# A difference of states moved from VectorE to GpSimd, and other starting constants for a planner, in a four-layer graph network

## The chip, the cores and the metric

The kernel runs on one core of one Trainium2 chip. A time is the device time of one execution in microseconds. The core has a matrix engine (TensorE, PE in the profile, with its weight loads as PEld), a vector engine (VectorE, DVE), a scalar engine (ScalarE, ACT), a programmable vector engine (GpSimd, POOL), and DMA queues that are issued here by SyncE (SP) and ScalarE.

## The reference

There are 64 graphs of 256 nodes with 256 features (`x`) and a 0/1 adjacency matrix (`adj`, about 1.6% ones). Four residual layers follow one another; each normalises the rows and takes `relu`:

```
h = max(layernorm(x), 0);  x = x + GAT0(h, adj)       # 4 heads, softmax over neighbours, elu
h = max(layernorm(x), 0);  x = x + GAT1(h, adj)       # 4 heads, relu, residual, layernorm by head
h = max(layernorm(x), 0);  x = x + GAT2(h, adj)       # one head
h = max(layernorm(x), 0);  x = x + GRU(h, adj)        # three rounds:
    m = h @ weight[i];  aggr = A^T m
    r = sigmoid(W_ir aggr + W_hr h + b)               # and z alike
    n = tanh(W_in aggr + b + r * (W_hn h + b))
    h = (1 - z) * n + z * h
```

All arithmetic is fp32.

## The kernel before

**Units.** The graphs are worked on in 33 units: one graph, then 31 units of two graphs, then one graph (`units`, L854). For each unit `graphs` (L1080) records every operation of the four layers. Nothing is issued at this point: an operation is an entry with an engine, a cost in ns, the buffers that it reads and writes, and a function that emits it.

**The planner.** `_Schedule` (L546) then orders all operations of all units. `paths` (L651) gives each operation a first due time, from the end that its unit should have (PACE per two graphs, L520 and L1666) backwards: the due time of a successor, less STRETCH times that successor's cost, less MARGIN. `play` (L712) runs a simple model of the engines forward. On each engine the operation with the earliest due time among those that are ready goes first; a result is visible on another engine OVERLAP and HOP ns after the producer is free again (L562, L563); an operation marked `port=True` starts only when no other such operation, of VectorE or GpSimd, is running in the model. `latest` (L664) plays the same backwards from the starts of the forward play, and its start times are the due times of the next forward play. After seven plays (ROUNDS) the best order by the model's own span is issued (`run`, L791), with the order on each engine fixed. So four of the five changed numbers (PACE, HOP, STRETCH, MARGIN) have no instruction of their own: they decide which order comes out.

**Pools.** Buffers come from pools of fixed size (L891 to L902): 13 of "g" (128x512 fp32), 8 PSUM banks, 3 of "sw" and so on. The model reserves them in its order.

**The GRU of a unit of two graphs.** In each of its three rounds, `products` (L1550) forms the sums for the gates r and z of both graphs from seven products of 128x512 in place of eight. It needs four differences, each 128x512 fp32 with both inputs in SBUF, made by `less_of` (L1566) on VectorE at a planned cost of 700 ns:

- t1 = state of graph 1 less state of graph 0 (L1593), from the state `ht` alone
- t3 = aggregate of graph 1 less state of graph 1
- t2 = aggregate of graph 1 less t1
- t4 = aggregate of graph 0 less t2

t1 goes into t2 and into the product with `s[0]`; t2 into t4 and the product with `s[1]`. All matmuls of `products` carry line 1575, all differences line 1567. The aggregate `ag` is made from the same state: transposes (`rows_of`, L1491), a split into high and low parts on ScalarE (L1450) and VectorE, 16 matmuls for each half (L1463), and a copy on ScalarE. Units of one graph use `plain` (L1515) and have no such differences.

**GpSimd before.** It computes the powers of the normalisations (L1110 and L1111 for the rows, L1400 and L1401 for layer 1's heads), the caps of the adjacency (L1334) and a memset (L1232). At the start it also forms some products for score columns (`score_column`, L971, recorded at L912 through the helper `vec`).

Of the kernel before, what the change touches and what calls it, by code (L numbers as in the profile page):

```python
# [516 lines left out]
SCORE_MAX = 40.0  # L517
SLOPES = (0.2, 0.01, 0.2)
SPREAD = 3
PACE = 93600  # L520


def _runs(numbers):
# [22 lines left out]
class _Schedule:  # L546
# [13 lines left out]

    ENGINES = ("pe", "act", "dve", "pool", "sp")
    OVERLAP = {"pe": 0, "act": 90, "dve": 80, "pool": 0, "sp": 0}  # L562
    HOP = {"pe": 370, "act": 240, "dve": 240, "pool": 270, "sp": 0}  # L563
    DMA_LATENCY = 2000
    DMA_RATE = 220.0
    DMA_AHEAD = 2000
    STRETCH = 3.79
    MARGIN = 500
    ROUNDS = 7

    def __init__(self, tc, pools):
# [8 lines left out]
    def buf(self, cls, shape, dtype=F32, tile=None):  # L580
        return _Buf(cls, shape, dtype, tile)

    def op(self, engine, cost, emit, reads=(), writes=(), takes=(), nbytes=0, port=False):
        o = _Op()
        o.engine, o.cost, o.port, o.emit, o.group, o.nbytes = engine, cost, port, emit, self.group, nbytes
        o.index, o.succs, o.preds, o.bufs, o.takes = len(self.ops), [], set(), [], []
        for written, items in ((False, reads), (True, writes)):
            for item in items:
                b, part = item if isinstance(item, tuple) else (item, None)
                if b not in o.bufs:  # L590
                    o.bufs.append(b)
                    b.users += 1
                if written and not b.const and b not in o.takes:
                    o.takes.append(b)
                keys = list(b.parts) if part is None else [k for k in (part, None) if k in b.parts]
                for k in keys:
                    writer, readers = b.parts[k]
                    if writer is not None:
                        o.preds.add(writer)
                    if written:  # L600
                        o.preds.update(readers)
                writer, readers = b.parts.get(part, (None, []))
                if written:
                    if part is None:
                        b.parts.clear()
                    b.parts[part] = (o.index, [])
                else:
                    b.parts[part] = (writer, readers + [o.index])
        for b in takes:
            if not b.const and b not in o.takes:  # L610
                o.takes.append(b)
        o.preds.discard(o.index)
        for p in o.preds:
            self.ops[p].succs.append(o)
        self.ops.append(o)
        return o
# [28 lines left out]
    def lag(self, o, s):  # L645

        if o.nbytes:
            return self.DMA_LATENCY + o.nbytes / self.DMA_RATE
        return 0 if o.engine == s.engine == "pe" else self.OVERLAP[o.engine] + self.HOP[o.engine]

    def paths(self):  # L651

        due = {}
        for o in reversed(self.ops):
            late = self.end[o.group]
            for s in o.succs:
                if s.group == o.group or o.group < 0:
                    late = min(late, due[s.index] - self.STRETCH * s.cost - self.MARGIN)
            if o.nbytes:
# [52 lines left out]
    def play(self, due):  # L712
# [10 lines left out]
        def post(t, kind, o):  # L723
            nonlocal count
            count += 1
            heapq.heappush(events, (t, count, kind, o))
# [17 lines left out]
        while True:  # L744
# [25 lines left out]
            while events and events[0][0] == clock:  # L770
                _, _, kind, o = heapq.heappop(events)
                if kind == "free":
# [5 lines left out]
                    else:  # L778
                        post(clock + self.OVERLAP[o.engine] + self.HOP[o.engine], "done", o)
                    if o.engine == "pe":  # L780
# [30 lines left out]
def _fast_path(  # L811
# [34 lines left out]
    nc = tc.nc  # L846
# [56 lines left out]
    buf, op = sched.buf, sched.op  # L903
# [4 lines left out]
    def bank(dtype=F32):  # L908
        return buf("bank", [P, S * 4 // mybir.dt.size(dtype)], dtype)

    def vec(fn, cost, *args, reads=(), writes=(), engine="dve", port=False, **kw):
        emit = lambda: fn(*[a() if callable(a) else a for a in args], **kw)  # L912
        op(engine, cost, emit, reads, writes, port=port)
# [7 lines left out]
    def dma(engine, nbytes, emit, reads=(), writes=(), takes=()):  # L921
        return op(engine, 450 if engine == "sp" else 320, emit, reads, writes, takes, nbytes)
# [157 lines left out]
    def graphs(u, first, nb):  # L1080
# [5 lines left out]
        def part_of(fixed):  # L1086
            return lambda cost: fixed + (cost - fixed) * nb / 2

        pe, act, dve, pool = part_of(0), part_of(200), part_of(130), part_of(130)
# [351 lines left out]
        def gru(pair):  # L1441
# [63 lines left out]
            ht = transposed(hn, "ht3_")  # L1505
# [3 lines left out]
            for i in range(L):  # L1509
# [40 lines left out]
                def products(i, ht, ag, wi):  # L1550

                    of = lambda b, g: b.tile[:, :, g * N : (g + 1) * N]
                    p1, t1, t2, t3, t4 = (buf("g", [P, DC, N]) for _ in range(5))
                    turn = buf("turn", [P, 1])
                    ps_s, ps_t, ps_w = (bank() for _ in range(3))
                    s = {}  # L1560
                    for k in (1, 0, 2):
                        s[k] = buf("sw", [P, DC, D])
                        o = dma("sp", 1 << 18, lambda k=k: nc.sync.dma_start(s[k].tile, sd[i][k]), [(B_sd, (i, k))], [s[k]])
                        sched.after(o, "sw")

                    def less_of(out, x_, y_, reads, takes=()):  # L1566
                        return op("dve", 700, lambda: nc.vector.tensor_tensor(  # L1567
                            out.tile, x_(), y_(), op=OP.subtract), reads, [out], takes, port=True)

                    def product(ps, w, B_w, view, reads, first=False, last=False):  # L1570

                        def emit():
                            for j in range(DC):
                                for dc in range(DC):
                                    nc.tensor.matmul(  # L1575
                                        ps.tile[:, j * N : (j + 1) * N],
                                        lhsT=w()[:, dc, j * P : (j + 1) * P], rhs=view()[:, dc],
                                        start=(first and j == 0 and dc == 0), stop=(last and dc == DC - 1),
                                        skip_group_check=True,
                                    )  # L1580

                        op("pe", 1725, emit, [reads, B_w], [ps])

                    def kept(out, ps):
                        vec(nc.scalar.copy, 600, lambda: out.tile.rearrange("p j n -> p (j n)"), lambda: ps.tile,
                            reads=[ps], writes=[out], engine="act")

                    def added(out, ps, also=()):
                        vec(nc.vector.tensor_tensor, 700, lambda: out.tile,
                            lambda: ps.tile.rearrange("p (j n) -> p j n", j=DC), lambda: out.tile,  # L1590
                            op=OP.add, reads=[ps, *also], writes=[out])

                    less_of(t1, lambda: of(ht, 1), lambda: of(ht, 0), [ht])  # L1593
                    product(ps_s, lambda: whh[:, :, Z_], B_whh, lambda: of(ht, 0), ht, first=True)
                    kept(p1, ps_s)
                    sched.after(less_of(t3, lambda: of(ag, 1), lambda: of(ht, 1), [ht, ag], [turn]), "turn")
                    less_of(t2, lambda: of(ag, 1), lambda: t1.tile, [t1, ag])
                    less_of(t4, lambda: of(ag, 0), lambda: t2.tile, [t2, ag])
                    product(ps_w, lambda: s3, B_s3, lambda: t3.tile, t3, first=True)
                    kept(t3, ps_w)  # L1600
                    product(ps_s, lambda: s[1].tile, s[1], lambda: t2.tile, t2)
                    kept(t2, ps_s)
                    product(ps_s, lambda: s[0].tile, s[0], lambda: t1.tile, t1)
                    added(t3, ps_s)
                    product(ps_w, lambda: wi[:, :, R_], B_wc, lambda: t4.tile, t4, last=True)
                    added(t2, ps_w, [turn])
                    product(ps_t, lambda: wi[:, :, Z_], B_wc, lambda: of(ag, 0), ag, first=True, last=True)
                    added(p1, ps_t)
                    product(ps_s, lambda: s[2].tile, s[2], lambda: of(ag, 1), ag, last=True)
                    return (t2, t3), p1, ps_s  # L1610
# [43 lines left out]
                ht = h_new  # L1654
# [9 lines left out]
    for u, (first, nb) in enumerate(units):  # L1664
        sched.group = u
        sched.end[u] = (first + nb) * PACE / 2  # L1666
        graphs(u, first, nb)
# [3 lines left out]
    sched.group = U  # L1671
    sched.end[U] = sched.end[-1] = (B / 2 + 1) * PACE
    good, bad = buf("rs", [P, 64]), buf("rs", [P, 1])
# [66 lines left out]
```

## Time and profile before

| | |
|---|---|
| median of three runs | 3055.6 us (3054.23 to 3055.82) |
| the profiled execution, its own time | 3056.75 us |
| its span, first to last instruction | 3054.7 us |
| mean granted TensorE clock | 0.993 |
| L1567 VectorE g<-ht (t1) | 93 operations, mean 681 ns, 63.3 us in all |
| L1567 VectorE, the other differences | 93 of g<-ag,ht and 186 of g<-ag,g, mean 680 ns |
| GpSimd, two-input operation 128x256 fp32 at the start | 684 to 728 ns |
| GpSimd, power operation 128x4 and 128x8 | mean 1130 and 1757 ns |

The times of rows come from one profiled execution. The mean of a row is the length of one instruction; neighbouring instructions on an engine overlap somewhat, so that VectorE's operations of 680 ns follow each other every 600 ns. "Idle before" in a row is time in which that engine had nothing running just before instructions of the row, and the arrow names what ended it. The helper `vec` records many operations under line 912, so they are told apart by the names of their buffers.

### The profile page before, as it was taken

What the parts mean: (1) busy time and instruction counts of PE and PEld (TensorE: products, weight loads), DVE (VectorE), ACT (ScalarE), POOL (GpSimd) and SP (SyncE); (2) the same over time, 40 slices, a digit from 0 to 9 for tenths busy, and PEclk for the clock granted to TensorE, in tenths of its full rate; (3) what the DMA queues carried; (4) which work ended last, traced back from release to release, by engine and by line L of the source; (5) the groups of instructions that cost most, each with busy time, mean ns of one, the idle gap of its engine ahead of it and who ended that gap; (6) DMA issues with size and microseconds to landing.
All of it is one profiled execution on the core that took longest, in us unless ns stands there. A gap on an engine that the chain in (4) does not pass through costs nothing.

```text
span 3054.7 us, 56348 instructions
## 1 busy us (share of the span) xinstructions
PE 3000.5 (98%) x20900; PEld 2370.9 (78%) x20900; DVE 2533.0 (83%) x5933; ACT 2109.2 (69%) x4811; POOL 430.3 (14%) x643
## 2 busy tenths in 40 slices
PE   8799999999999999999999999999999999999998
PEld 7677787777787777787777787777777777787777
DVE  7876878888988888988888988888988888988764
ACT  7676667767776767766767766767776766766554
POOL 3311101111111111111111111111111111101100
PEclk9899999999999999999999999999999999999999
DMA  4111222221222122222121222221222221121110
GB/s 139 59 50 47 69 67 90 61 81 59 81 81 77 60 80 60 80 81 76 61 80 58 82 81 73 63 81 56 84 80 70 66 81 57 60 79 56 45 49 24
DMA packets 150936, 212.43 MB, mean 70 GB/s; under 512 B 49239, under 2 KB 102013, under 8 KB 143229
## 3 DMA queue, kind: packets, MB, share of 16 engines
q1 hardware_dynamic: 146752, 207.40, 21.7%
q8 instruction: 167, 2.74, 0.4%
q10 hardware_dynamic: 3900, 1.34, 0.2%
q14 instruction: 117, 0.95, 0.1%
HBM read 180.62 MB, written 19.68 MB: 66 GB/s over the span
## 4 chain that ended last, share of the span: by engine, by line
PE 95%; DVE 2%; ACT 1%; DMA 1%; issue 0%; POOL 0%; SPq 0%; ACTq 0%; DVEq 0%
PE bank L1575 37%; PE bank L1477 23%; PE bank L1267 12%; PE bank L1158 11%; PE bank L1463 6%; PE bank L1136 4%; PE bank L1491 3%; PE bank L1195 1%; DVE pt L912 1%; DVE g L912 0%; DVE o L912 0%; PE bank L1211 0%; PE bank L1032 0%; ACT g L912 0%; DMA xt<-in_x_dram 0%
## 5 line engine op out<-in xcount | busy, mean ns | idle before, releaser
L912 ACT ACTIVATE g<-g,bg 128x256 f32<-128x256 f32 (+1 forms) x756 | 393.9, 555 | 164.4 <-DVE g L912 96.6
L912 DVE SCALAR_TENSOR_TENSOR pt<-pt,f,cap 128x256 f32<-128x256 f32 x1152 | 476.2, 479 | 11.9 <-ACT pt L1248 10.1
L1248 ACT ACTIVATE pt<-cb,f 128x256 f32<-128x256 f32 x1062 | 441.3, 504 | 4.2 <-PE bank L1267 3.7
L1267 PEld LDWEIGHTS bank<-wh,pt 128*64 128x64 f32 (+1 forms) x8704 | 345.5, 141 | 85.5 <-issue 62.3
L1267 PE MATMUL bank<-wh,pt 128*64 128x65 f32 (+1 forms) x8704 | 391.3, 233 | 6.5 <-DVE pt L912 2.7
L912 DVE TENSOR_TENSOR g<-bank,g 128x512 f32<-128x512 f32 x279 | 191.4, 686 | 241.6 <-PE bank L1575 234.3
L1477 PE MATMUL bank<-ht,whh 128*128 128x512 f32 (+1 forms) x888 | 379.4, 561 | 0.0
L1477 PE MATMUL bank<-ag,wc 128*128 128x512 f32 (+1 forms) x888 | 377.9, 558 | 0.1
L1575 PE MATMUL bank<-g,sw 128*128 128x256 f32 x1488 | 349.8, 381 | 2.7 <-DVE g L1567 2.7
L912 DVE SCALAR_TENSOR_TENSOR g<-g,g 128x512 f32<-128x512 f32 (+1 forms) x396 | 257.2, 670 | 80.7 <-ACT g L912 80.5
L1575 PEld LDWEIGHTS bank<-g,sw 128*128 128x128 f32 x1488 | 278.7, 190 | 44.9 <-issue 4.5
L912 ACT ACTIVATE g<-bank,bg 128x256 f32<-128x256 f32 (+1 forms) x408 | 224.6, 568 | 108.3 <-PE bank L1477 97.6
L912 ACT COPY g<-bank 128x512 f32<-128x512 f32 x279 | 162.6, 583 | 187.8 <-PE bank L1575 181.9
L1477 PEld LDWEIGHTS bank<-ag,wc 128*128 128x128 f32 x888 | 164.4, 190 | 129.1 <-issue 120.1
L1477 PEld LDWEIGHTS bank<-ht,whh 128*128 128x128 f32 x888 | 161.1, 190 | 122.3 <-issue 103.6
L1463 PE MATMUL bank<-am_r,hl 128*128 128x256 f32 x1536 | 233.7, 301 | 0.0
L1119 ACT ACTIVATE xn<-xt,mv 128x256 f32<-128x256 f32 x384 | 210.5, 597 | 24.6 <-DVE mv L912 22.9
L1463 PEld LDWEIGHTS bank<-am_r,hl 128*128 128x128 f32 x1536 | 196.2, 189 | 31.8 <-issue 21.7
L1101 DVE BATCH_NORM_STATS2 st<-xt 128x6 f32<-128x256 f32 x512 | 207.9, 406 | 10.1 <-DMA xt<-in_x_dram 9.9
L912 ACT COPY ht<-bank 128x512 f32<-128x512 f32 (+1 forms) x264 | 143.4, 575 | 101.5 <-PE bank L1136 101.3
L1110 POOL TENSOR_SCALAR mv<-mv 128x4 f32<-128x4 f32 (+1 forms) x132 | 48.3, 366 | 1152.1 <-DVE mv L1102 1029.6
L1575 PE MATMUL bank<-ht,whh 128*128 128x256 f32 x744 | 180.2, 386 | 0.4 <-ACT ht L912 0.4
(113 smaller groups left out, 5389.9 us busy)
## 6 DMA issues: line engine op xcount, KB each, us to landing
sw<-sd SPq DMA_DIRECT2D x279, 256.0 KB, 2.7
cb<-rd SPq DMA_DIRECT2D x58, 1024.0 KB, 4.7
xt<-in_x_dram SPq DMA_DIRECT2D x31, 512.0 KB, 4.0
at<-in_adj_dram SPq DMA_DIRECT2D x31, 512.0 KB, 3.8
out_dram<-xt SPq DMA_DIRECT2D x31, 512.0 KB, 2.9
cb<-rd SPq DMA_DIRECT2D x29, 256.0 KB, 3.3
sd<-g SPq DMA_DIRECT2D x9, 256.0 KB, 2.3
cap<-cap_n SPq DMA_TRANSPOSE x128, 2.3
```

Source lines behind the costliest of these rows:

```text
L912: emit = lambda: fn(*[a() if callable(a) else a for a in args], **kw)
L1101: nc.vector.bn_stats(st.tile[:, c, :], xt.tile[:, c, :])
L1110: nc.gpsimd.tensor_scalar(mv.tile[:, 2, :], mv.tile[:, 1, :], 1e-5, None, op0=OP.add)
L1119: op("act", 610, lambda: nc.scalar.activation(xn.tile[:, c, :], xt.tile[:, c, :], AF.Relu, bias=mv.tile[:, 3, c : c + 1], scale=mv.tile[:, ...
L1136: nc.tensor.transpose(ps.tile[:, c * P : (c + 1) * P], xn.tile[:, c, dc * P : (dc + 1) * P], ident)
L1158: nc.tensor.matmul(ps.tile[:, : heads * W], lhsT=ht.tile[:, dc, c * P : (c + 1) * P], rhs=we[:, dc].rearrange("p h w -> p (h w)"), start=( ...
L1248: op("act", 500, lambda: nc.scalar.activation(pt.tile[:, b, jc, :], source(h, b), AF.Exp, scale=slope - 1.0, bias=f.tile[:, 1, h, c : c + ...
L1267: nc.tensor.matmul(ps[q * Q : (q + 1) * Q], lhsT=pt.tile[:, b, jc, i0 : i0 + Q], rhs=wh.tile[:, h, 2 * b + jc, :w], start=(jc == 0), stop= ...
L1463: nc.tensor.matmul(ps.tile[:, b * N : (b + 1) * N], lhsT=hl.tile[:, k, 2 * b + sc, :], rhs=am.tile[:, 2 * b + sc, :], start=(k == 0 and sc ...
L1477: nc.tensor.matmul(ps.tile[:, :S], lhsT=w[:, dc, g * P : (g + 1) * P], rhs=v.tile[:, dc, :], start=(first and dc == 0), stop=(last and dc ...
L1491: nc.tensor.transpose(ps.tile[:, c * P : (c + 1) * P], ht.tile[:, j, c * P : (c + 1) * P], ident)
L1575: nc.tensor.matmul(ps.tile[:, j * N : (j + 1) * N], lhsT=w()[:, dc, j * P : (j + 1) * P], rhs=view()[:, dc], start=(first and j == 0 and d ...
```

## The change

One of the four differences (t1) is computed by GpSimd with a planned cost of 1290 ns; the other three stay on VectorE. Four constants of the planner are different.

```diff
-PACE = 93600
+PACE = 94400
...
-    HOP = {"pe": 370, "act": 240, "dve": 240, "pool": 270, "sp": 0}
+    HOP = {"pe": 340, "act": 210, "dve": 210, "pool": 240, "sp": 0}
...
-    STRETCH = 3.79
-    MARGIN = 500
+    STRETCH = 3.33
+    MARGIN = 800
...
-                    def less_of(out, x_, y_, reads, takes=()):
-                        return op("dve", 700, lambda: nc.vector.tensor_tensor(
+                    def less_of(out, x_, y_, reads, takes=(), engine="dve"):
+                        eng = nc.vector if engine == "dve" else nc.gpsimd
+                        return op(engine, 700 if engine == "dve" else 1290, lambda: eng.tensor_tensor(
                             out.tile, x_(), y_(), op=OP.subtract), reads, [out], takes, port=True)
...
-                    less_of(t1, lambda: of(ht, 1), lambda: of(ht, 0), [ht])
+                    less_of(t1, lambda: of(ht, 1), lambda: of(ht, 0), [ht], engine="pool")
```

## The prediction

> **What bounds the kernel now.** I read the page's busy shares first, then the stages, then who waits for whom.
>
> ```profile
> span 3054.7 us, 56348 instructions
> PE 3000.5 (98%) x20900; PEld 2370.9 (78%) x20900; DVE 2533.0 (83%) x5933; ACT 2109.2 (69%) x4811; POOL 430.3 (14%) x643
> ...
> PE 95%; DVE 2%; ACT 1%; DMA 1%; issue 0%; POOL 0%; SPq 0%; ACTq 0%; DVEq 0%
> ```
>
> TensorE is idle for 3054.7 - 3000.5 = 54.2 us in the whole span, and the chain that ended last is 95% TensorE. A matmul's end is modelled, so "busy" alone would not prove that TensorE is the limit. The view of stages says where the 54 us are (columns: stage, its length, busy time and instructions of each engine, granted clock, DMA share, GB/s):
>
> ```profile
> 0.00:86.00 86.00, 69.71 (x784) 60.83 (x784) 63.13 (x192) 60.69 (x170) 23.37 (x49) 1.00 0.43 124
> 86.00:108.00 22.00, 5.15 (x38) 3.47 (x39) 19.91 (x57) 4.67 (x10) 10.96 (x10) 0.54 0.04 14
> 108.00:206.00 98.00, 98.00 (x701) 80.29 (x701) 77.91 (x210) 77.22 (x188) 19.02 (x31) 0.98 0.22 68
> 206.00:350.00 144.00, 133.93 (x937) 107.55 (x938) 113.51 (x278) 87.53 (x206) 21.07 (x31) 0.96 0.21 64
> 350.00:2800.00 2450.00, 2449.93 (x17113) 1928.41 (x17113) 2086.58 (x4827) 1746.54 (x3958) 339.29 (x498) 1.00 0.23 72
> 2800.00:3047.00 247.00, 243.03 (x1330) 189.96 (x1328) 169.82 (x369) 132.53 (x283) 16.63 (x24) 0.99 0.12 36
> 3047.00:3055.00 8.00, 0.75 (x4) 0.40 (x4) 2.15 (x7) 0.00 (x0) 0.00 (x0) 0.72 0.33 108
> ```
>
> Idle of TensorE: 16.3 us before 86 (nearly all of it the first loads), 16.9 in 86 to 108, 10.1 in 206 to 350, 4.0 and 7.0 at the end. Between 350 and 2800 it is 0.07 us in 2450. The list of waits, restricted to TensorE and to 500 to 2780, comes back empty. The same pattern of matmuls comes round every 91.8 us there (76 matmuls of L1267 start at 1061.95, 1153.74 and 1245.55 in the chain), and that is the matmul work of a unit of two graphs: nothing but fewer or faster matmuls would shorten this part, and the change touches no matmul. So only the filling and the draining can gain. The filling has one large hole (timeline, TensorE then GpSimd; the bracket is the idle time before the piece and its releaser):
>
> ```profile
> 88.10 1.22 PE L1267 MATMUL bank<-wh,pt 128*64 128x65 f32 x16 [0.52 <-DVE pt L912]
> 104.12 2.80 PE L1136 MATMUL bank<-ident,xn 128*128 128x128 f32 x8 [14.80 <-ACT xn L1119]
> ...
> 86.06 0.20 POOL L1400 TENSOR_SCALAR mean<-mean 128x8 f32<-128x8 f32 x1 [10.27 <-DVE mean L912]
> ...
> 89.64 2.98 POOL L1400 TENSOR_SCALAR mean<-mean 128x8 f32<-128x8 f32 x1 [1.64 <-DVE mean L912]
> ```
>
> In the hole VectorE is 91% busy (19.91 of 22.00) with the second layer's normalisation of the first units, and TensorE waits for what follows from it. The last two lines are one instruction, 0.20 us and then 2.98 us: in the second case VectorE issued five operations with two SBUF inputs back to back (89.47 to 92.55 in its timeline), and GpSimd ended 0.1 us after them.
>
> **What the Trainium skill says.** "SBUF — State Buffer", section "Who interferes with whom": VectorE's second SBUF read port is GpSimd's only one; an operation of VectorE with two SBUF inputs and a GpSimd operation that reads SBUF exclude each other for whole instructions, and whoever starts first holds it. The 2.98 us agree. "GPSIMD Engine Reference", section 3.1: a two-input elementwise operation takes 4497 ns at 2048 fp32 elements, 2.2 ns each, about twice VectorE's. The trace agrees: 684 ns on GpSimd at 256 elements. "TensorE: Matmul & The Clock Gate", Part 1: after an idle window of some 3.4 us the clock is halved until TensorE has been busy for as long. The granted clock of 0.54 in 86 to 108 agrees, and 16 matmuls of L1158 take 5.86 us at 107.39 where they take 3.56 at 115.02: the hole costs 2.3 us more than its idle time.
>
> **The change, part by part.**
>
> *t1 to GpSimd.* Of the row "L1567 DVE TENSOR_TENSOR g<-ht ... x93 | 63.3, 681" all 93 leave VectorE. They start 0.60 us apart from the next operation (1383.18 to 1383.78), so VectorE gets back 93 x 0.60 = 56 us, 1.8 us per unit of 91.8. GpSimd gets 93 operations of 128x512. No row shows one; from 684 ns plus 256 x 2.2 ns I estimate 1.25 us, and the planner's 1290 ns lie beside it. That is 116 us more on GpSimd, 430 to 546 us, 18% of the span. While it holds the port, VectorE's two-input operations wait: at worst 1.25 us each time, 3.75 us per unit. VectorE therefore changes by -1.8 to +1.95 us per unit; it is busy 78.8 us in 500 to 592, so it ends between 77 and 81 of 92. TensorE stays the limit by 11 us per unit. In latency, t1 is 0.6 us longer alone and up to 3 us when the port is taken (the 2.98 above). What waits for t1 is t2 and then two products; t2 also needs the aggregate of the new state, which takes transposes, a split and 16 matmuls after the same state. At 1419.16 a t1 is done and the next t2 comes at 1427.60. So I take 0 for 350 to 2800. Bounds: nothing below 0, as TensorE has nothing to gain there; above, see the rival D. Behind a t1 in GpSimd's queue stand the power operations of the normalisations; they wait up to 1.25 us more, and in the full part other matmuls cover that.
>
> In 206 to 350, where TensorE waited 2.7 us for an L1567 operation and 2.8 for hl, four t1 stand: 4 x 0.60 = 2.4 us of VectorE. A third to a half is on TensorE's path: -1 us. In 86 to 108 there is no t1 (the first starts at 144.3): nothing.
>
> *HOP 30 ns lower.* This alters no instruction, only the planner's idea of a latency. It is safe when the chip is faster than the plan: a copy on ScalarE starts 0.19 us after the matmul slots of its group are over (68.99 against 67.93 + 4 x 0.217), and the plan had 0.37 and gets 0.34. So no new waits from it: 0.
>
> *PACE, STRETCH, MARGIN.* They set only the due times of the first of seven plays; from then on due times come from the previous order. An operation of cost c moves its predecessors' due time by 3.79c + 500 before and 3.33c + 800 after. The two are equal at 300 / 0.46 = 652 ns, which is a usual cost on VectorE: a matmul group of 1725 ns pulls 0.49 us less, one of 160 ns 0.23 us more. PACE moves the units' ends 0.8 us further apart per unit. So it is a small push to a procedure that settles into a different order. Direct cost 0; what it does is redraw the filling and the draining. Here I can't work out the order by hand, only what is at stake. To be gained: the hole (16.9 idle + 2.3 of slow clock), 10.1 in 206 to 350, about 4 before the end, and 1.9 of the last 7.0 (one wait, the rest is the last rows and their DMA): 35 us at most. To be lost: any number, in steps such as the one in rival C. For the hole: VectorE had 4 us free in 50 to 62 (7.76 of 12.00) and then was full from 74 on, and two of GpSimd's operations stood in the chain for 4.6 us with the port taken. An order that takes the first, single graph ahead, or spreads that normalisation, halves it. I put -9 on this, half of 19.2 rounded down, and nothing on the end.
>
> *Sum.* 0 (full part) - 1 - 9 + 0 = -10. Span 3054.7 - 10 = 3044.7. The profiled run took 3056.75, 2.05 more than its span; the median of the runs is 1.15 less than that one. 3044.7 + 2.05 - 1.15 = 3045.6, so **3046 us** as a median.
>
> **Rivals.**
>
> A, the forecast, faster by over 0.2%: between the bound (3049.5) and nearly all of the 35 us, 3025 to 3049. For it: there are 31 us that depend on order alone, and VectorE, relieved, is what the hole waits for. Against: the relief itself starts after the hole.
>
> B, a redrawn order with the same holes: 3050 to 3061, middle 3055. For it: the units' needs at the start are the same, so VectorE must do the early layers before TensorE has a GRU to fill with. Against: 20 us of holes rarely come out the same within 6.
>
> C, slower, the filling: one more normalisation of layer 1 comes ahead of what TensorE waits for. One half is nine VectorE operations at 0.60 and two GpSimd ones (0.54 + 1.76): 7.7 us, two halves 15.4. All of it is TensorE's idle time, as in 89 to 104. That gives 3071, and it decides once TensorE's ready work at about 90 us is used up, which in the profile before it was at 89.3. Seen against it: the planner knows these costs; for it: it knows nothing of GpSimd locked out for 2.98 us.
>
> D, slower, in the full part: t1 starves behind VectorE's runs of two-input operations, or stops them, and a product waits in every layer. If 0.65 us each time (1.25 - 0.60) were uncovered, 93 x 0.65 = 60 us: 3116. It needs the cushion of several us to be gone; the empty list of waits speaks against it.
>
> **How the numbers follow.** A measurement of this kernel tells a change from none at about 0.2%, 6.1 us (3049.5 and 3061.7 are the bounds). Chances: A 0.45, B 0.20, C 0.29, D 0.06. Faster 0.45, same 0.20, slower 0.35. The likeliest one's own range is 3030 to 3049. Both signs hold most of the chance, so the range reaches from 3028, below which I leave A's best tenth or so, to 3078, above which are D and the cases of C with more than three such halves.
>
> **What would show it.** Right: TensorE idle of about 44 us, the stage up to 350 shorter, the spacing of the pattern still 91.8 us, L1567 with 93 operations on GpSimd of 1.2 to 1.4 us by median. Wrong in the part on t1: waits of TensorE for a GpSimd or L1567 release in the middle, or GpSimd operations of 3 us there. Wrong in the part on the order: the hole near 90 us longer than 15, or a new hole in the last 250 us.

## The result and the profile after

The changed kernel takes 3042.85 us (median of five, 3041.36 to 3043.07) against 3055.54 us for the kernel before in the same comparison: a ratio of 0.9958, 95% interval 0.9946 to 0.9969. That is 12.7 us less; 3046 had been forecast. The span went from 3054.7 to 3041.3 us, so 13.4 us are to be found in the profile.

The busy shares on the page of the kernel after:

```profile
span 3041.3 us, 56441 instructions
PE 2994.3 (98%) x20900; PEld 2369.7 (78%) x20900; DVE 2505.3 (82%) x5840; ACT 2111.0 (69%) x4811; POOL 541.3 (18%) x736
```

93 instructions went from VectorE to GpSimd. TensorE's idle time fell from 54.2 to 47.0 us (span less busy), that is by 7.2. Its busy time fell by 6.2 although its 20900 matmuls are the same. The stages (stage, its length, busy time and instructions of each engine, granted clock, DMA share, GB/s), kernel after:

```profile
0.00:86.00 86.00, 69.62 (x743) 59.98 (x744) 59.34 (x186) 58.87 (x167) 22.26 (x49) 1.00 0.42 124
86.00:108.00 22.00, 6.53 (x79) 4.64 (x78) 20.20 (x56) 5.63 (x12) 7.83 (x8) 0.67 0.00 0
108.00:206.00 98.00, 98.00 (x701) 80.37 (x702) 82.56 (x221) 80.08 (x194) 23.64 (x36) 0.99 0.24 75
206.00:350.00 144.00, 141.14 (x1080) 113.37 (x1081) 113.04 (x276) 95.67 (x223) 24.37 (x32) 1.00 0.21 63
350.00:2800.00 2450.00, 2449.52 (x17040) 1932.04 (x17037) 2073.55 (x4772) 1748.25 (x3960) 437.37 (x582) 1.00 0.22 72
```

Read against the same stages before, idle time is length less the first busy number. In 206 to 350 it is 2.9 us where it was 10.1: all of the 7.2 us by itself. The hole in 86 to 108 is 15.5 us where it was 16.9, and the end after 2800 is 0.8 us longer (11.8 against 10.9). The clock column explains the busy time. In 206 to 350 the granted clock was 0.96 and is now 1.00. The clock record of the trace has three stretches of 3.41 us at half clock there before, from 214.10, 234.58 and 326.74 on, and none after. Each began within 1.5 us of the end of one of the small waits (timeline, TensorE, kernel before; the bracket is the wait):

```profile
212.69 1.11 PE L1267 MATMUL bank<-wh,pt 128*128 128x257 f32 x4 [1.88 <-DVE o L912]
234.19 3.43 PE L1575 MATMUL bank<-g,sw 128*128 128x256 f32 x8 [2.67 <-DVE g L1567]
325.91 0.66 PE L1491 MATMUL bank<-ident,ht 128*128 128x128 f32 x4 [2.75 <-DVE hl L912]
```

At half clock a stretch costs half its length, 3 x 1.7 = 5.1 us. Behind the hole, TensorE worked at half clock for 7.6 us before and for 5.6 us after, worth 1.0 us. Together that is 6.1 of the 6.2 us.

So of 13.4 us, 12.3 come from 206 to 350 (7.2 of idle time and 5.1 of slow clock), 2.4 from the hole, and about 1.3 are given back in the full part and at the end. The hole itself still stands (timeline, TensorE, kernel after; the bracket is the idle time and its releaser):

```profile
92.00 0.57 PE L1267 MATMUL bank<-wh,pt 128*64 128x65 f32 x12 [1.25 <-DVE pt L912]
105.11 2.81 PE L1136 MATMUL bank<-ident,xn 128*128 128x128 f32 x8 [12.54 <-ACT xn L1119]
```

and t1 looks as was estimated (instructions of the line of the differences, which is L1568 here because the change adds a line above it; durations in ns as least, median, most):

```profile
L1568 POOL TENSOR_TENSOR g<-ht x93: 1262/1273/2834, 140.5 to 2978.0; 128x512 f32<-128x512 f32 x93
```

What the profile can't say is which part of the change did it: t1's engine, or the constants by way of the order. In the kernel before, TensorE waited 2.7 us for an L1567 operation just in the stage that gained, which makes relief of VectorE a tempting answer.

### The profile page after: what moved, and what is told of

The parts are those of the page before. It is cut to its first block, busy times and chain, and to the rows that moved or that the text cites. A ratio compares the mean times of both kernels' runs of the same rounds, so it can differ in the third digit from the quotient of the medians.

```text
span 3041.3 us, 56441 instructions
## 1 busy us (share of the span) xinstructions
PE 2994.3 (98%) x20900; PEld 2369.7 (78%) x20900; DVE 2505.3 (82%) x5840; ACT 2111.0 (69%) x4811; POOL 541.3 (18%) x736
## 4 chain that ended last, share of the span: by engine, by line
PE 96%; DVE 2%; ACT 1%; DMA 1%; issue 0%; SPq 0%; POOL 0%; ACTq 0%; DVEq 0%
PE bank L1576 37%; PE bank L1477 23%; PE bank L1267 12%; PE bank L1158 11%; PE bank L1463 6%; PE bank L1136 4%; PE bank L1491 3%; PE bank L1195 1%; ACT pt L1248 1%; PE bank L1211 0%; DVE g L912 0%; DVE pt L912 0%; PE bank L1032 0%; ACT g L912 0%; DMA xt<-in_x_dram 0%; DVE o L912 0%
## 5 line engine op out<-in xcount | busy, mean ns | idle before, releaser
L912 ACT ACTIVATE g<-g,bg 128x256 f32<-128x256 f32 (+1 forms) x756 | 396.9, 558 | 186.9 <-DVE g L912 110.7
L912 DVE SCALAR_TENSOR_TENSOR pt<-pt,f,cap 128x256 f32<-128x256 f32 x1152 | 479.0, 479 | 9.7 <-ACT pt L1248 6.1
L1248 ACT ACTIVATE pt<-cb,f 128x256 f32<-128x256 f32 x1062 | 449.3, 505 | 33.9 <-PE bank L1267 32.6
L912 DVE TENSOR_TENSOR g<-bank,g 128x512 f32<-128x512 f32 x279 | 191.2, 686 | 258.4 <-PE bank L1576 251.6
L1267 PEld LDWEIGHTS bank<-wh,pt 128*64 128x64 f32 (+1 forms) x8704 | 346.5, 141 | 66.5 <-issue 34.9
L1267 PE MATMUL bank<-wh,pt 128*64 128x65 f32 (+1 forms) x8704 | 386.0, 232 | 3.4 <-DVE pt L912 2.5
L1477 PE MATMUL bank<-ht,whh 128*128 128x512 f32 (+1 forms) x888 | 386.0, 563 | 0.8 <-ACT ht L912 0.8
L1477 PE MATMUL bank<-ag,wc 128*128 128x512 f32 (+1 forms) x888 | 373.1, 558 | 0.0
L912 ACT ACTIVATE g<-bank,bg 128x256 f32<-128x256 f32 (+1 forms) x408 | 230.4, 567 | 188.2 <-PE bank L1477 166.0
L912 DVE SCALAR_TENSOR_TENSOR g<-g,g 128x512 f32<-128x512 f32 (+1 forms) x396 | 260.3, 671 | 76.2 <-ACT g L912 76.1
L1477 PEld LDWEIGHTS bank<-ag,wc 128*128 128x128 f32 x888 | 164.5, 190 | 139.3 <-issue 121.7
L912 ACT COPY g<-bank 128x512 f32<-128x512 f32 x279 | 162.6, 583 | 140.3 <-PE bank L1576 127.5
L1568 POOL TENSOR_TENSOR g<-ht 128x512 f32<-128x512 f32 x93 | 123.5, 1328 | 764.0 <-DVE ht L912 369.7
L1477 PEld LDWEIGHTS bank<-ht,whh 128*128 128x128 f32 x888 | 159.6, 190 | 107.1 <-issue 94.3
L1110 POOL TENSOR_SCALAR mv<-mv 128x4 f32<-128x4 f32 x132 | 43.1, 326 | 1009.0 <-DVE mv L1102 555.9
L912 ACT COPY ht<-bank 128x512 f32<-128x512 f32 (+1 forms) x264 | 143.5, 574 | 88.2 <-PE bank L1136 87.7
```

Of the source, the lines that this page charges most:

```text
L1248: op("act", 500, lambda: nc.scalar.activation(pt.tile[:, b, jc, :], source(h, b), AF.Exp, scale=slope - 1.0, bias=f.tile[:, 1, h, c : c + ...
L1267: nc.tensor.matmul(ps[q * Q : (q + 1) * Q], lhsT=pt.tile[:, b, jc, i0 : i0 + Q], rhs=wh.tile[:, h, 2 * b + jc, :w], start=(jc == 0), stop= ...
L1477: nc.tensor.matmul(ps.tile[:, :S], lhsT=w[:, dc, g * P : (g + 1) * P], rhs=v.tile[:, dc, :], start=(first and dc == 0), stop=(last and dc ...
L1568: return op(engine, 700 if engine == "dve" else 1290, lambda: eng.tensor_tensor(out.tile, x_(), y_(), op=OP.subtract), reads, [out], takes ...
```

## The experiments

Theory R (redraw): the gain is the order that the planner happened to find; the constants and the engine of t1 are only seeds for it. Theory V (relief): VectorE's freed time brings the gain. Theory K: the constants bring it by themselves. "Model" in the expectations is the span that the kernel's own planner gives to the order that it issues. Idle times of TensorE below are stage length less busy time. The diffs of e1, e2 and e4 to e8 are against the changed kernel, those of e3, e9, e10 and e12 against the kernel before. Each ratio is to the kernel before on the same chip.

**e1_consts: the new constants, t1 on VectorE.**

```diff
-                    less_of(t1, lambda: of(ht, 1), lambda: of(ht, 0), [ht], engine="pool")
+                    less_of(t1, lambda: of(ht, 1), lambda: of(ht, 0), [ht])
```

> The new PACE, HOP, STRETCH and MARGIN, with t1 still on VectorE. Theory R (redraw: the gain is the order that the planner happened to find, and the filling decides it): the planner's own model gives 3073.4 us here against 3050.0 for the changed kernel, so some 10 to 20 us slower than the changed kernel on the chip, 3053 to 3065, with TensorE idle of 55 us or more. Theory V (relief: VectorE's 56 us freed bring the gain): as before, 3054 to 3057, because the constants do nothing by themselves. Theory K (the constants bring it): 3043.

Measured: 3067.27 us, ratio to the kernel before 1.0044 (1.0027 to 1.0060), just above the range of R. TensorE idles 64.4 us, of which 8.3 are between 350 and 2800. V (no effect) and K (all of the gain) both fail.

**e2_pool: t1 on GpSimd, the old constants.**

```diff
-PACE = 94400
+PACE = 93600
...
-    STRETCH = 3.33
-    MARGIN = 800
+    STRETCH = 3.79
+    MARGIN = 500
```

HOP is back at its old values as well.

> t1 on GpSimd with the old PACE, HOP, STRETCH and MARGIN. R: the model gives 3102.5 against 3071.6 for the kernel before, so slower than before by 10 to 30 us, 3065 to 3085. V: most of the gain is here, 3043 to 3047. K: as before, 3055.

Measured: 3082.59 us, ratio 1.0093 (1.0076 to 1.0110). Each part alone makes the kernel slower, by 13 and 28 us, and both together make it faster by 13: they don't add. The stage that was full is not full here:

```profile
350.00:2800.00 2450.00, 2421.64 (x16811) 1896.56 (x16810) 2056.00 (x4692) 1708.63 (x3888) 474.70 (x573) 1.00 0.22 71
```

28.4 us of TensorE are idle in it. VectorE's 2056.00 us there look freer than the 2086.58 of the kernel before, but the stage also holds 1.8% fewer matmuls, so less work passed through it. Over the whole span VectorE is busy for 2525.8 us against 2533.0: only 7 us of the 56 that the prediction counted were freed. So e2 is no test of relief; e4 is one, beside the changed kernel: the same order with t1 on either engine.

**e3_order_before and e4_order_after: the engine alone, with the order held.** In e3 t1 is planned as before (VectorE, 700 ns) and emitted on GpSimd:

```diff
-                    def less_of(out, x_, y_, reads, takes=()):
-                        return op("dve", 700, lambda: nc.vector.tensor_tensor(
+                    def less_of(out, x_, y_, reads, takes=(), eng=nc.vector):
+                        return op("dve", 700, lambda: eng.tensor_tensor(
...
+                    less_of(t1, lambda: of(ht, 1), lambda: of(ht, 0), [ht], eng=nc.gpsimd)
```

In e4 it is planned as in the changed kernel (GpSimd, 1290 ns) and emitted on VectorE:

```diff
-                        eng = nc.vector if engine == "dve" else nc.gpsimd
+                        eng = nc.vector
```

> The order of the kernel before, as planned for VectorE, but t1 is emitted on GpSimd at its place in that order. R: 3054 to 3057, the same waits of TensorE as before, because the relief is not on its path; 350 to 2800 still without idle time. V: 3043 to 3050, the stage 206 to 350 loses 5 us or more of idle time. Rival D of the prediction (t1 starves in the full part): 3060 or more, with idle time of TensorE after 350.

> The order of the changed kernel, as planned for GpSimd, but t1 is emitted on VectorE at its place in that order. R: within 2 us of the changed kernel, 3042 to 3046. V: most of the gain goes, 3050 to 3056, with VectorE late in 206 to 350.

e4 measured 3046.43 us (ratio 0.9974, 0.9964 to 0.9983), just above the range of R (3042 to 3046). With t1 back on VectorE, 8 of 13 us stay by the ratios (0.9974 against 0.9958), and the stage that gained is unchanged:

```profile
206.00:350.00 144.00, 141.02 (x1086) 113.55 (x1082) 115.08 (x281) 95.46 (x223) 17.91 (x27) 1.00 0.20 62
350.00:2800.00 2450.00, 2447.82 (x17004) 1928.53 (x17003) 2099.17 (x4843) 1742.71 (x3959) 332.51 (x502) 1.00 0.22 72
```

3.0 us of idle time in the first line, against 2.9 in the changed kernel. So the order closed the small holes, not the relief. The engine is worth some 2 to 5 us in this order (2.3 by the spans of the two profiles, 3.6 by the medians, 5 by the ratios); in the profiles 1.7 us of TensorE's idle time lie in the full part and 1.4 at the end.

e3 measured 3093.74 us (ratio 1.0128, 1.0111 to 1.0145). I had R at 3054 to 3057; it is rival D of the prediction that came. The waits of TensorE between 350 and 2800 in e3, where the kernel before has none (waiting line, the line waited for: us in total, times, longest):

```profile
PE bank L1158 <- DVE g L912: 29.1, 19, 1.6
```

The timelines of VectorE and GpSimd in one period of e3 show how:

```profile
1592.59 0.69 DVE L1567 TENSOR_TENSOR g<-ag,g 128x512 f32<-128x512 f32 x1 [2.16 <-POOL g L1567]
```

```profile
1588.59 0.57 POOL L1400 TENSOR_SCALAR mean<-mean 128x8 f32<-128x8 f32 x1 [0.70 <-DVE mean L912]
1589.24 2.07 POOL L1401 TENSOR_TENSOR mean<-mean,nhalf 128x8 f32<-128x8 f32 x1
1591.29 1.27 POOL L1567 TENSOR_TENSOR g<-ht 128x512 f32<-128x512 f32 x1
```

t1 stands in GpSimd's queue right behind a power operation of 2.07 us, which itself waited for VectorE; the t2 on VectorE stands still 2.16 us for it, everything behind t2 on VectorE is late by as much, and that includes the additions that read products out of PSUM. TensorE then waits 1.57 us at its next matmul group, L1158 at 1601.31, for such an addition (in the trace its releaser is "DVE g L912"). That happens once per unit in 19 of the units, 29 us in all. The pattern comes every 93.64 us there, against 91.80 in the kernel before.

**e12_rounds_1_2: is it that one place in the queue?** The planned order shows that in the steady pattern only the t1 of GRU round 0 comes right after a power operation of layer 1. So it alone goes back to VectorE:

```diff
-                    less_of(t1, lambda: of(ht, 1), lambda: of(ht, 0), [ht], eng=nc.gpsimd)
+                    less_of(t1, lambda: of(ht, 1), lambda: of(ht, 0), [ht], eng=nc.gpsimd if i else nc.vector)
```

> As e3_order_before, but t1 goes to GpSimd only in the GRU rounds 1 and 2; in round 0 it stays on VectorE. In e3's steady pattern the t1 of round 0 stands in GpSimd's queue right behind a power operation of layer 1, and t2 waits 2.16 us for it. Theory Q (that one place in the queue makes the loss): the 29 us of TensorE's waits on L1158 go, 3054 to 3060. Theory P (each t1 on GpSimd costs alike, by the shared port): two thirds of the 38 us stay, 3077 to 3085.

Measured: 3058.64 us, ratio 1.0011 (1.0002 to 1.0019). Of the 39 us that e3 lost, 36 are gone with a third of the moved operations, and TensorE has no wait between 350 and 2800 again. Theory Q holds; P falls. The other 62 on GpSimd cost some 3 us together and gain nothing.

**e5_hop_old and e6_pace_94300: how fine is the draw?** The changed kernel with one constant changed in each.

```diff
-    HOP = {"pe": 340, "act": 210, "dve": 210, "pool": 240, "sp": 0}
+    HOP = {"pe": 370, "act": 240, "dve": 240, "pool": 270, "sp": 0}
```

```diff
-PACE = 94400
+PACE = 94300
```

> The changed kernel with HOP alone back at 370/240/240/270. Theory R (each set of constants draws another order, and the planner's own model ranks the orders): the model gives 3057.9 us against 3050.0 for the changed kernel, of which some are only the longer latencies, so 3043 to 3052 on the chip. If the lower HOP itself is what brings the gain (plans nearer to the chip), 3053 or more.

> The changed kernel with PACE 94300 in place of 94400, t1 still on GpSimd. R: the model gives 3087.3 us, 37 more than for the changed kernel, so slower than the kernel before, 3065 to 3085, with idle time of TensorE between 350 and 2800. If t1 on GpSimd or the direction of the constants brings the gain, a change of 0.1% in one of them does nothing: 3041 to 3045.

Measured: 3049.76 us (0.9980, 0.9971 to 0.9988) and 3066.54 us (1.0037, 1.0023 to 1.0050), both as R has it. A change of PACE by 0.1% costs 24 us, more than the whole gain and in the other direction. There is no "better PACE"; there is an order that was found with 94400.

**e7_seed and e8_seed_hop: other sets for the changed kernel.** e7 has PACE 94700, STRETCH 3.7, MARGIN 550; e8:

```diff
-PACE = 94400
+PACE = 94500
...
-    HOP = {"pe": 340, "act": 210, "dve": 210, "pool": 240, "sp": 0}
+    HOP = {"pe": 280, "act": 150, "dve": 150, "pool": 180, "sp": 0}
...
-    STRETCH = 3.33
-    MARGIN = 800
-    ROUNDS = 7
+    STRETCH = 3.4
+    MARGIN = 450
+    ROUNDS = 9
```

> The changed kernel with PACE 94700, STRETCH 3.7 and MARGIN 550, the best of some 380 random sets by the planner's own model at this HOP (3043.6 us, 6.4 below the changed kernel's). R: 3036 to 3043, with the hole near 90 us or the filling up to 350 shorter. If the chip doesn't follow the model within a few us: 3043 to 3055.

> The changed kernel with HOP 280/150/150/180, PACE 94500, STRETCH 3.4, MARGIN 450 and nine plays in place of seven: model 3039.8 us, of which the shorter latencies alone may be 15. R: 3040 to 3052. If plans with latencies nearer to the chip's 0.2 us are better plans: 3030 to 3040. If they are too tight: TensorE idles between 350 and 2800, over 3055.

Measured: 3040.63 us (0.9951, 0.9937 to 0.9964) and 3036.73 us (0.9935, 0.9920 to 0.9951). e7 is within the range of R. e8 is below it, in the range put there for the rival that a HOP nearer to the chip's latencies makes better plans by itself. In e8 the hole in 86 to 130 is down to 11.0 us, and in e7 to 14.1.

**e9_dve_seed, e10_dve_seed_hop, e11_after_again: is GpSimd needed at all?** The kernel before, t1 on VectorE, with other constants. e9:

```diff
-PACE = 93600
+PACE = 93900
...
-    HOP = {"pe": 370, "act": 240, "dve": 240, "pool": 270, "sp": 0}
+    HOP = {"pe": 280, "act": 150, "dve": 150, "pool": 180, "sp": 0}
...
-    STRETCH = 3.79
+    STRETCH = 3.68
```

e10 goes on to HOP 240/110/110/140, STRETCH 3.31, MARGIN 850 and eight plays; e11 is the changed kernel as it is.

> The kernel before, t1 on VectorE, with HOP 280/150/150/180, PACE 93900, STRETCH 3.68, MARGIN 500: the best set at this HOP of 260 random ones for this placement by the planner's own model (3036.7 us; e8_seed_hop, with t1 on GpSimd and the same HOP, had 3039.8 and 3036.7 on the chip). Theory R (only the order counts, and VectorE has orders as good): 3031 to 3041. If GpSimd is needed for such an order (VectorE, 2 us per unit fuller, idles TensorE in places): over 3045.

> t1 on VectorE, HOP 240/110/110/140, PACE 93900, STRETCH 3.31, MARGIN 850, eight plays: the lowest model span of all (3034.8). R, with latencies in the model still no shorter than the chip's: 3030 to 3042. If HOP is now too short for the chip: idle time of TensorE between 350 and 2800, 3045 or more.

> The changed kernel once more, beside these two on one chip: 3040 to 3045.

Measured on one chip: e9 3027.18 us (ratio to the kernel before 0.9908, 0.9893 to 0.9923), e10 3044.61 us (0.9967, 0.9955 to 0.9979), e11 3042.26 us (0.9960, 0.9945 to 0.9975). e9 beats the kernel before by 27.6 us and the changed one by 15, with not one instruction on another engine: only the order differs from the kernel before. VectorE carries all of t1 and is busy for 84% of the span, and it does no harm. The time is 4 us below the range of R. The page of e9, and its stages:

```profile
span 3025.6 us, 56382 instructions
PE 2986.2 (99%) x20900; PEld 2369.9 (78%) x20900; DVE 2538.8 (84%) x5933; ACT 2100.5 (69%) x4811; POOL 435.8 (14%) x643
```

```profile
86.00:108.00 22.00, 11.95 (x75) 8.78 (x76) 20.03 (x62) 7.38 (x17) 9.25 (x11) 0.61 0.14 47
108.00:206.00 98.00, 96.48 (x700) 79.39 (x698) 81.57 (x211) 76.74 (x185) 18.88 (x29) 1.00 0.21 63
206.00:350.00 144.00, 142.66 (x1101) 114.28 (x1101) 116.15 (x289) 97.76 (x227) 18.90 (x27) 1.00 0.22 65
350.00:2800.00 2450.00, 2448.48 (x17096) 1936.50 (x17096) 2107.89 (x4871) 1742.85 (x3971) 350.07 (x506) 1.00 0.24 72
```

Here the hole, 10.1 us in the first line, is what the prediction had hoped for. e10 missed its range, and not as expected: idle time in 350 to 2800 is only 1.6 us. The last section takes that up.

Two things follow from these sets together. First, the rival about HOP stays open. e8 and e9, with HOP 90 ns below the kernel before, are the fastest, and e5, with HOP alone raised again, loses 7 us against the changed kernel; but e8 and e9 change other constants too, e5 is a single draw, and the lowest HOP (e10) is not the fastest. Second, the planner's model, which needs no chip, ranks the orders well. It gives 3071.6 us for the kernel before, 3050.0 for the changed one, 3073.4, 3102.5, 3057.9, 3087.3, 3043.6, 3039.8 and 3036.7 for e1, e2 and e5 to e9. The chip ranks these nine alike, except that e1 and e6 change places, 1 us apart. Only e10, the lowest in the model (3034.8), falls out of line. e7 and e9 were the best in the model of some 380 and 260 random sets, so their lead comes from a search and not from one draw.

TensorE's idle time by stage, from the stages of each profile (us; before 86, 86 to 130, 130 to 350, 350 to 2800, after 2800):

| kernel | median | idle before 86 | hole | to 350 | full part | end |
|---|---|---|---|---|---|---|
| before | 3055.5 | 16.3 | 16.9 | 10.1 | 0.1 | 10.9 |
| after | 3042.9 | 16.4 | 15.5 | 2.9 | 0.5 | 11.8 |
| e1, constants alone | 3067.3 | 16.4 | 18.0 | 10.1 | 8.3 | 11.6 |
| e2, GpSimd alone | 3082.6 | 15.3 | 16.5 | 4.6 | 28.4 | 10.7 |
| e3, old order, GpSimd | 3093.7 | 16.2 | 17.3 | 11.9 | 30.0 | 11.5 |
| e4, new order, VectorE | 3046.4 | 16.4 | 15.1 | 3.2 | 2.2 | 13.2 |
| e8 | 3036.7 | 16.9 | 11.0 | 2.9 | 3.2 | 10.4 |
| e9 | 3027.2 | 15.6 | 10.2 | 2.7 | 1.5 | 9.4 |

## Why the prediction was right, and where its steps were not

- **That only filling and draining could gain, and that the constants act only through the order:** right for this change. The gain lies before 350 us, the pattern goes on at 91.77 us per unit (91.80 before), and e4, e6 and e9 show that the order is the cause. As a rule it is wrong: in e9 another order of the same matmuls shortens the period itself to 91.48 us (last section). The prediction said that it couldn't work out the order; the planner's model, which it didn't ask, gives 21.6 us less for the change, where the chip has 12.7.
- **t1 on GpSimd, cost:** 1.25 us estimated, 1273 ns measured by median. VectorE in 500 to 592 was put at 77 to 81 of 92; it is 77.96.
- **t1's worth, -1 us in 206 to 350, by relief:** wrong in cause. With the order held (e4) that stage loses nothing when t1 returns to VectorE. The direct worth, 2 to 5 us in this order, lies in the full part and at the end, which the prediction put at 0. The relief was also smaller than 56 us: VectorE's busy time fell from 2533.0 to 2505.3, by 28.
- **-9 us from the hole near 90 us:** mis-sized. It gave 2.4 with its clock, and at 15.5 us it is still longer than the 15 that the prediction named as the sign of being wrong there. The holes in 206 to 350, of which the sum took 1, gave 12.3. The sum, -10 against -13.4 of span, was near only because two terms were wrong in opposite directions: that the number was right is luck.
- **Slow clock:** it was priced for the hole and left out for the small waits, because the prediction had the clock halved after an idle window of some 3.4 us. Three shorter waits, of 1.9 to 2.8 us, were each followed by a half-clock stretch of 3.41 us in the kernel before, 1.7 us on top of each wait. It isn't certain for each such wait: in e3 the first of them is longer (below, timeline, TensorE), and the clock record has no slow stretch after it. In the hole the price of 2.3 us was too low: the slow clock began at 87.81, before the long wait, and TensorE worked for 7.6 us at half clock behind it, which costs 3.8.

```profile
215.44 1.11 PE L1267 MATMUL bank<-wh,pt 128*128 128x257 f32 x4 [2.88 <-DVE o L912]
```

- **"The cushion of several us" of t1 (rival D, 0.06):** there is no such cushion in the old order. It was read from one t1 at 1419.16; another of the same pattern, at 1385.05, has its t2 0.60 us later. e3 lost 39 us. The price of 60 us for D was reckoned for three t1 per unit, and one of them did it (e12). D didn't happen in the changed kernel, whose order was planned with t1 on GpSimd. But planning for it is not enough: e2 was planned so too and has 28 us of idle time in the full part.
- **Rival C (slower through the filling):** a longer hole was seen in e1 and e6 (18.0 and 20.5 us), 1 to 4 us longer and not the 15 put there.

What the runs don't settle: why this order has almost no waits in 206 to 350, in terms of single operations. The two orders differ nearly everywhere, so no single swap was tried. Nor do they settle what a lower HOP is worth by itself, or which operations make the 28 us of waits in e2, which are spread over many lines.

## What to carry to other kernels

When a planner or a list of due times orders the work, an edit of its constants or of one cost is a new draw of the whole order: compare the two engines with the order held fixed before a gain is put down to the engine. An operation moved to a nearly idle engine is not free: it stands in that engine's queue in the order of another plan, and one place behind a 2 us operation cost 36 us here, while the freed time on an engine that wasn't the limit was worth 2 to 5. And when the bounding engine is 98% busy, look for the few small waits that are left, with the slow clock that can follow them, and for other orders; e9 got twice the gain of the change with no edit to the work. Let the planner's model choose among orders first, and let the chip decide among the best, since the model's own best (e10) was not the chip's.

## What the runs showed of the hardware that was not expected

**A full TensorE is not a fixed pace.** I took 91.8 us per unit as the matmul work itself. In e9 it is less, and in e10 more, at the same matmuls and the same clock of 1.00. Pieces that come round once per unit in the chain that ended last (start, length, what), e9 and then e10:

```profile
433.07 3.88 PE bank L1267 x128
524.54 3.88 PE bank L1267 x128
616.01 3.89 PE bank L1267 x128
```

```profile
709.61 3.63 PE bank L1477 x8
...
801.63 3.63 PE bank L1477 x8
...
893.65 3.63 PE bank L1477 x8
```

That is 91.47 (91.48 on average) against 92.02 us: 0.5 us per unit, some 14 us over 27 units, which is nearly all of the 14.6 us between the spans of e9 and e10. Against the kernel before (91.80) the shorter period is worth some 8 of the 27.6 us that e9 gains. Two things in the starts of the matmuls account for most of it. The 65-column matmuls of L1267 follow each other every 30 ns on average, but the first of them after a group of another line starts 93 ns late (522 against 429 after L1477, 309 against 216 after L1575), and the first matmul of another line after them 120 ns late (150 against 30). A separate visit to L1267 so costs 0.21 us; e9 makes three per unit, the kernels before and after and e10 four. The rest are waits of 50 to 100 ns at the start of a group, which the modelled end of the group ahead covers, so that they count as busy: about 0.5 us per unit in e10, 0.2 in e9. A HOP too short for the chip isn't shown as their cause: counted in the same way, the kernel before has 0.4 with the longest HOP, and e8 0.5 with the same HOP as e9.

**A power operation on GpSimd can take twice its time in the hole.** In the kernel after, the one at 91.70 took 3.55 us and the one at 88.03 took 1.66. The long one began during a run of VectorE's two-input operations (91.48 to 93.76) and ended 1.5 us after that run, while VectorE stood idle for 1.53 us until it was done. That fits the lock on the shared port that the prediction used; no run tried it alone.
